# Seven biases moved off TensorE, an earlier switch of ScalarE's order, and another order for the last stores

## The chip, the cores and the metric

The kernel runs on one core of one Trainium2 chip. The metric is the device time of one execution in microseconds (us). The kernel before takes 311.48 us, the median of 3 runs (311.41 to 311.85). One execution was profiled; it took 311.45 us, and its profile spans 309.7 us from the first instruction to the last.

## The reference

There are 128 batches. Each is a matrix of 128 rows by 512 columns in 32-bit floats, and each has an integer that picks one of 10 sets of weights. The reference does this for every batch:

```python
w1 = W1[language_ids]                      # 10 x 512 x 128
w2 = W2[language_ids]                      # 10 x 128 x 512
h = einsum('bsh,bha->bsa', hidden_states, w1) + b1[language_ids][:, None, :]
h = relu(h)
adapted = einsum('bsa,bah->bsh', h, w2) + b2[language_ids][:, None, :]
x = hidden_states + adapted
normed = (x - mean(x)) * rsqrt(var(x) + 1e-05)      # over the 512 columns
return normed * gamma[language_ids][:, None, :] + beta[language_ids][:, None, :]
# and the whole is: x_in + that
```

The kernel has to form, per batch, a down-projection to 128 columns, a ReLU, an up-projection back to 512 columns, the residual sum with the bias b2, a layer norm with gamma and beta, and a second residual sum.

## The kernel before

**One batch at a time, five engines in a pipeline.** A batch fills one tile of 128 partitions by 512 columns. All weights stay in SBUF; biases, gamma and beta are spread over the 128 partitions once at the start (`spread`, L201). The main loop turns i from 3 to 129, and each turn handles several batches at different stages. With b = i - 3, a turn issues in this order:

- TensorE (PE) transposes batch i in four pieces (`transpose_x`, L234, tile pxT), multiplies batch i - 1 down (`down`, L257, tile ph) and multiplies batch i - 2 up (`up`, L274, tile py).
- GpSimd (POOL) forms r = x + b2 for batch b + 2 (`add_b2`, L244) and writes x + beta for batch b into the output tile o (`add_beta`, L251). Tile r has a ring of four buffers, o a ring of five buffers of two batches each.
- ScalarE (ACT) copies the transposed batch i out of PSUM (`copy_xT`, L238), applies the ReLU to batch i - 1 (`relu`, L265), copies the weights of batch i + 1 into place (`stage_w1`, L225), and squares batch b with a row sum (`square`, L310). After every second square it takes a reciprocal root for the pair of batches (`root`, L320).
- VectorE (DVE) adds r (or x) to py with a row sum (`residual`, L291), applies mean and gamma to an earlier batch (`scale`, L353), finishes a still earlier batch into o (`finish`, L362), and runs short steps on single columns in between (L298, L324, L326, L329).
- SyncE (SP) issues the loads of x (L71) and the stores of finished pairs (`store`, L366).

**Three ways to add b2.** In most batches GpSimd adds b2 to x ahead of time (`add_b2`) and VectorE's residual reads r. In the batches named by `b2_by_matmul` TensorE adds it, with one short matmul ahead of the up-projection into the same PSUM tile (L273), and residual reads x. In those named by `b2_by_vector` VectorE adds it to py with an instruction of its own (`vector_b2`, L284), and residual reads x.

Here B is 128 and E is B - 5 = 123. By these rules 15 batches go by matmul before (0, 1, 2, 3, 5, 9, 17, 30, 46, 62, 78, 94, 110, 121, 123), 20 by VectorE and 93 by GpSimd.

**What sets the order.** `keep` pins each engine's instructions to the order in which the program issues them; each engine works through its own list, and waits in front of an instruction whose inputs or buffers aren't ready. `stage_w1` has two places in the loop: ahead of the square from LATE on, and behind the square and the root for the batches from FIRST (8) to LATE - 1:

```python
if i + 1 >= LATE and on(i + 1):
    stage_w1(i + 1)
...
if FIRST <= i + 1 < LATE:
    stage_w1(i + 1)
```

**The tail.** From batch 124 on `tail` (L421) takes the place of the paired steps. Batches 124 to 127 get a root of their own, and each is stored on its own (`store_last`, L415). For batches 123 and 124, `by_pool` gives ScalarE the normalization (L408) and GpSimd the product with gamma (L410) and the sum with o (L412). Batch 125 is split: VectorE finishes the right 256 columns (`finish_cols`, L419), ScalarE and GpSimd the left 256 (L408, L412). Batches 126 and 127 are finished by VectorE (L419).

Of the kernel before, what the change touches and what calls it, by code (L numbers as in the profile page):

```python
# [18 lines left out]
EPS = 1e-5  # L19
FIRST = 8  # L20
EARLY = 24
LATE = 20
U = 2


# [1 line left out]
def cond_resid_kernel(ctx: ExitStack, tc: tile.TileContext, x, itok, W1, b1, W2, b2, gamma, beta, out):  # L27
# [8 lines left out]
    nc = tc.nc  # L36
    B, S, H = x.shape
# [8 lines left out]
    def keep(ins):  # L46

        engine = ins.ins.engine
        if engine in last:
            tc.add_manual_dep(ins.ins, last[engine], behind, reason="kept order")  # L50
        last[engine] = ins.ins.name
        return ins
# [14 lines left out]
    E = B - 5  # L67
# [65 lines left out]
    def lid(b, engine):  # L133
        g = b // G
        if (g, engine) not in lids:
            loads, vals = nc.values_load_multi_w_load_instructions(
                lang[0:1, g * G : (g + 1) * G],
                engines=[engine],
                min_val=0,
                max_val=L - 1,  # L140
                skip_runtime_bounds_check_because="clamped on the chip to 0..L-1 above",
            )
            for ins in loads:
                keep(ins)
            lids[g, engine] = vals
        return lids[g, engine][b % G]
# [65 lines left out]
    xT, hT, rs, os, ys, ssqs, nmeans, rstds = {}, {}, {}, {}, {}, {}, {}, {}  # L212
# [1 line left out]


    def b2_by_matmul(b):
        return b in (0, 1, 2, 3, 5, E - 2, E) or (b % 8 == 1 if b < 24 else b % 16 == 14 and b < E)

    def b2_by_vector(b):
        return 8 <= b < B - 8 and (b % 8 == 5 if b < 24 else b % 16 in (1, 6, 11))  # L220

    def stage_w1(b):
        w1s[b] = wp.tile([P, KC, A], FP, tag="w1s", name=f"w1s_{b}")
        src = (w1e if b < EARLY else w1).rearrange("p l k a -> p (l k a)")[:, bass.ds(lid(b, ET.Activation) * (KC * A), KC * A)]
        keep(nc.scalar.copy(w1s[b].rearrange("p k a -> p (k a)"), src))  # L225
# [37 lines left out]
    def relu(b):  # L263
        hT[b] = tp.tile([P, P], FP, tag="hT", name=f"hT_{b}", bufs=6)
        keep(nc.scalar.activation(hT[b], phs.pop(b), AF.Relu, bias=b1T[:, bass.ds(lid(b, ET.Activation), 1)]))  # L265
# [11 lines left out]
    def col(tiles, b):  # L277

        return tiles[b // 2][:, b % 2 : b % 2 + 1]
# [6 lines left out]
    def residual(b):  # L286
        r = rs.pop(b) if b in rs else xb(b)
        if b % 2 == 0:
            sums[b // 2] = st.tile([P, 2], FP, tag="sum", name=f"sum_{b // 2}")
        keep(  # L290
            nc.vector.scalar_tensor_tensor(ys[b], ys[b], 1.0, r, ALU.mult, ALU.add, accum_out=col(sums, b))  # L291
        )

    def negative_means(g):

        nmeans[g] = st.tile([P, 2], FP, tag="nmean", name=f"nmean_{g}")
        keep(
            nc.vector.scalar_tensor_tensor(  # L298
                nmeans[g], sums[g], -1.0 / H, ys[2 * g + 1][:, 0:2], ALU.mult, ALU.bypass
            )  # L300
        )
# [20 lines left out]
    def newton(n, ssq, t, u):  # L322
        if n == 1:
            keep(nc.vector.scalar_tensor_tensor(u, ssq, EPS * H3, t, ALU.add, ALU.mult))  # L324
        else:
            keep(nc.vector.scalar_tensor_tensor(u, u, 1.0 / H3, t, ALU.mult, ALU.mult))  # L326

    def newton_3(rstd, t, u):
        keep(nc.vector.scalar_tensor_tensor(rstd, u, -3.0, t, ALU.add, ALU.mult))  # L329
# [8 lines left out]
    def deviation(g):  # L338
        root(ssqs[g], of_pair(g)[0])

    def rstd(g, n):
        t, u = of_pair(g)
        if n < 3:
            newton(n, ssqs[g], t, u)
        else:
            rstds[g] = st.tile([P, 2], FP, tag="rstd", name=f"rstd_{g}")
            newton_3(rstds[g], t, u)
            del ssqs[g], parts_of[g]

    def scale(b):  # L350
        v = lid(b, ET.DVE)
        keep(
            nc.vector.scalar_tensor_tensor(  # L353
                ys[b], ys[b], col(nmeans, b), gamma_b[:, bass.ds(v * H, H)], ALU.add, ALU.mult
            )
        )

    def finish(b):
        g, j = divmod(b, 2)
        o = os[g][:, j, :]  # L360
        keep(
            nc.vector.scalar_tensor_tensor(o, ys.pop(b), rstds[g][:, j : j + 1], o, ALU.mult, ALU.add)  # L362
        )

    def store(g):
        keep(nc.sync.dma_start(out=out[2 * g : 2 * g + 2].rearrange("b s h -> s b h"), in_=os.pop(g)))  # L366
        del rstds[g]

    def on(b):
        return 0 <= b < B  # L370
# [5 lines left out]
    def of_one(b):  # L376
        if -b not in parts_of:
            pool, tag = {E + 3: (p_h, "h"), E + 4: (p_x, "xT")}.get(b, (p_s, "s"))
            parts_of[-b] = pool.tile([P, 1], FP, tag=tag, name=f"root_of_{b}"), st.tile([P, 1], FP, tag="part", name=f"part_of_{b}")
        return parts_of[-b]  # L380

    def rstd_of(b, n):

        t, u = of_one(b)
        if n < 3:
            newton(n, ssqs[b], t, u)
        else:
            rstds[b] = st.tile([P, 1], FP, tag="rstd", name=f"rstd_{b}")
            newton_3(rstds[b], t, u)

    def deviation_of(b):
        ssqs[b] = st.tile([P, 1], FP, tag="ssq", name=f"ssq_{b}")
        sq = tp.tile([P, H], FP, tag="sq", name=f"sq_{b}")
        keep(nc.scalar.activation(sq, ys[b], AF.Square, bias=col(sums, b), scale=-float(H), accum_out=ssqs[b]))
        root(ssqs[b], of_one(b)[0])
# [4 lines left out]
    def shift(b):  # L400
        shifts[b] = st.tile([P, 1], FP, tag="shift", name=f"shift_{b}")
        keep(nc.vector.tensor_scalar(shifts[b], col(nmeans, b), rstd_col(b), None, ALU.mult))

    def by_pool(b, scaled, cols=slice(0, H)):

        n = rp.tile([P, H], FP, tag="r", name=f"n_{b}")[:, cols]
        bias = 0.0 if scaled else shifts[b]
        keep(nc.scalar.activation(n, ys[b][:, cols], AF.Identity, bias=bias, scale=rstd_col(b)))  # L408
        if not scaled:
            keep(nc.gpsimd.tensor_tensor(n, n, gamma_b[:, bass.ds(lid(b, ET.Pool) * H, H)], ALU.mult))  # L410
        o = os[b // 2][:, b % 2, cols]
        keep(nc.gpsimd.tensor_tensor(o, n, o, ALU.add))  # L412

    def store_last(b):
        nc.sync.dma_start(out=out[b], in_=os[b // 2][:, b % 2, :])  # L415

    def finish_cols(b, cols=slice(0, H)):
        o = os[b // 2][:, b % 2, cols]
        keep(nc.vector.scalar_tensor_tensor(o, ys[b][:, cols], rstd_col(b), o, ALU.mult, ALU.add))  # L419

    def tail(b):  # L421
        p = E // 2
        residual(b)
        if b == E + 1:
            rstd(p, 1)
            scale(E - 1)
            rstd(p, 2)
            finish(E - 2)
            store(p - 1)
            rstd(p, 3)  # L430
            deviation_of(b)
            shift(E)
            by_pool(E, False)
        elif b == E + 2:
            rstd_of(b - 1, 1)
            negative_means(b // 2)
            rstd_of(b - 1, 2)
            finish_cols(E - 1)
            store_last(E - 1)
            rstd_of(b - 1, 3)  # L440
            store_last(E)
            deviation_of(b)
        elif b == E + 3:
            left, right = slice(0, H // 2), slice(H // 2, H)
            shift(b - 2)
            by_pool(b - 2, False)
            residual(b + 1)
            store_last(b - 2)
            rstd_of(b - 1, 1)
            scale(b - 1)  # L450
            rstd_of(b - 1, 2)
            negative_means(b // 2)
            deviation_of(b)
            scale(b)
            rstd_of(b - 1, 3)
            rstd_of(b, 1)
            deviation_of(b + 1)
            rstd_of(b, 2)
            scale(b + 1)
            rstd_of(b, 3)  # L460
            rstd_of(b + 1, 1)
            finish_cols(b - 1, right)
            by_pool(b - 1, True, left)
            store_last(b - 1)
            rstd_of(b + 1, 2)
            finish_cols(b)
            store_last(b)
            rstd_of(b + 1, 3)
            finish_cols(b + 1)
            store_last(b + 1)  # L470
# [46 lines left out]
    for i in range(3, B + U):  # L517
        b = i - U - 1
# [19 lines left out]
        if i > 4 and on(i - 1):  # L538
            relu(i - 1)
        if i + 1 >= LATE and on(i + 1):  # L540
            stage_w1(i + 1)
# [39 lines left out]
        if 0 <= b <= E:  # L581
            square(b)
            if half == 1:
                deviation(g)
        if FIRST <= i + 1 < LATE:
            stage_w1(i + 1)
# [41 lines left out]
```

## Time and profile before

| what | value |
|---|---|
| median of 3 runs | 311.48 us (311.41 to 311.85) |
| the profiled execution | 311.45 us, span 309.7 us |
| busy: PE | 297.2 us (96%) |
| busy: DVE | 294.7 us (95%) |
| busy: ACT | 280.5 us (91%) |
| busy: POOL | 279.6 us (90%) |
| granted TensorE clock, mean | 0.987 |
| moved by DMA | 77.59 MB, mean 251 GB/s |

The page's busy time is the union of the instructions' spans, and an instruction's span on VectorE and ScalarE laps over the start of the next one by some 0.07 to 0.1 us. So the cost of one more instruction on a full engine is the distance from its start to the start of the next one, which is a little less than the mean duration that the groups list. Four engines are above 90%, and the mean over the span doesn't tell which of them holds up the others; that has to be read from the waits and from the gaps in each engine's own timeline.

### The profile page before, as it was taken

To read this page: it belongs to the slowest core of one execution; us is meant where nothing else is said; L and a number is where in the kernel's file an instruction comes from. 1 tells how busy PE (TensorE), PEld (TensorE's weight loads), DVE (VectorE), ACT (ScalarE), POOL (GpSimd) and SP (SyncE) were. 2 spreads that over 40 slices of the span, in tenths; PEclk is the share of its full clock that TensorE was granted. 3 is DMA by queue.
4 is the path that set the end of the run, shared out by engine and by line. 5 is a ranking of instruction groups with operands and counts; after the bars stand their busy time and mean duration, and the time that the engine had idled before them with its cause. 6 is when DMAs were issued, how large, how long until landed. Compare 5 with 4: busy or idle time off the path is not lost.

```text
span 309.7 us, 6996 instructions
## 1 busy us (share of the span) xinstructions
PE 297.2 (96%) x1849; PEld 221.7 (72%) x1849; DVE 294.7 (95%) x823; ACT 280.5 (91%) x716; POOL 279.6 (90%) x234
## 2 busy tenths in 40 slices
PE   7999999999999999999999999999999999999960
PEld 3758777777777777777777777777777777777730
DVE  6787999999999999999999999999999999999994
ACT  3857999999999999999999999999999999999981
POOL 1349999988999999999999999999999999989962
PEclk9999999999999999999999999999999999999995
DMA  6999979976678666766777656667867666783334
GB/s 236 390 388 387 370 231 363 375 265 227 247 272 265 224 210 220 251 234 232 272 270 237 217 203 238 258 211 275 264 225 247 206 224 238 237 267 137 131 121 158
DMA packets 43482, 77.59 MB, mean 251 GB/s; under 512 B 1930, under 2 KB 7061, under 8 KB 43443
## 3 DMA queue, kind: packets, MB, share of 16 engines
q1 hardware_dynamic: 43382, 77.10, 71.2%
q8 instruction: 15, 0.25, 0.3%
q14 instruction: 25, 0.20, 0.2%
q10 hardware_dynamic: 60, 0.05, 0.1%
HBM read 43.58 MB, written 33.55 MB: 249 GB/s over the span
## 4 chain that ended last, share of the span: by engine, by line
PE 92%; DVE 4%; issue 1%; ACT 1%; DMA 1%; ACTq 0%; DVEq 0%
PE ph L257 36%; PE py L274 35%; PE pxT L234 18%; PE row L205 2%; PE py L273 1%; DVE py L353 1%; DVE py L291 1%; DVE o L419 1%; DMA rows<-in_L_cond_b_dram 1%; DVE b_b L210 0%; DVE left L186 0%; DVE left L184 0%; ACT sq L310 0%; DVE o L362 0%; ACT w1s L225 0%
## 5 line engine op out<-in xcount | busy, mean ns | idle before, releaser
L251 POOL TENSOR_TENSOR o<-x,beta_b 128x512 f32<-128x512 f32 x128 | 161.9, 1277 | 9.5 <-DVE beta_b L210 9.4
L257 PE MATMUL ph<-xT,w1s 128*128 128x128 f32 x1024 | 135.4, 275 | 0.0
L274 PE MATMUL py<-w,hT 128*128 x256 | 131.3, 594 | 0.2 <-ACT hT L265 0.2
L244 POOL TENSOR_TENSOR r<-x,b_b 128x512 f32<-128x512 f32 x93 | 118.7, 1276 | 11.8 <-DVE b_b L210 6.2
L257 PEld LDWEIGHTS ph<-xT,w1s 128*128 128x128 f32 x1024 | 124.9, 192 | 1.0 <-ACT hT L265 0.5
L234 PEld LDWEIGHTS pxT<-ident,x 128*128 128x128 f32 x512 | 66.3, 152 | 65.8 <-issue 35.7
L353 DVE SCALAR_TENSOR_TENSOR py<-py,nmean,gamma_b 128x512 f32<-128x512 f32 x126 | 94.9, 753 | 0.1
L310 ACT ACTIVATE sq<-py,sum 128x512 f32<-128x512 f32 x124 | 86.0, 693 | 5.4 <-DVE nmean L298 2.9
L362 DVE SCALAR_TENSOR_TENSOR o<-py,rstd,o 128x512 f32<-128x512 f32 x122 | 90.8, 744 | 0.0
L234 PE MATMUL pxT<-ident,x 128*128 128x128 f32 x512 | 78.1, 275 | 0.1
L238 ACT COPY xT<-pxT 128x512 f32<-128x512 f32 x128 | 74.7, 584 | 1.2 <-PE pxT L234 1.2
L291 DVE SCALAR_TENSOR_TENSOR py<-py,r 128x512 f32<-128x512 f32 x93 | 64.3, 692 | 2.7 <-PE py L274 1.2
L225 ACT COPY w1s<-w 128x512 f32 x104 | 64.0, 615 | 0.0
L265 ACT ACTIVATE hT<-ph,b1T 128x128 f32<-128x128 f32 x128 | 47.2, 369 | 6.6 <-PE ph L257 3.8
L274 PEld LDWEIGHTS py<-w,hT 128*128 128x128 f32 x256 | 39.9, 192 | 2.5 <-ACT hT L265 1.1
L291 DVE SCALAR_TENSOR_TENSOR py<-py,x 128x512 f32<-128x512 f32 x35 | 24.4, 697 | 2.0 <-PE py L274 0.9
L310 ACT ACTIVATION_READ_ACCUMULATOR sq<-py,sum 128x1 f32 x124 | 25.3, 204 | 0.0
L320 ACT ACTIVATE root<-ssq,eps 128x2 f32<-128x2 f32 x62 | 16.5, 266 | 2.1
L284 DVE TENSOR_TENSOR py<-py,b_b 128x512 f32<-128x512 f32 x20 | 13.8, 692 | 0.2
L291 DVE DVE_READ_ACCUMULATOR py<-py,r 128x1 f32 x93 | 13.1, 141 | 0.0
L225 ACT COPY w1s<-w1e 128x512 f32 x16 | 9.8, 611 | 1.1 <-DMA w1e<-in_L_cond_W_dram 1.1
L324 DVE SCALAR_TENSOR_TENSOR part<-ssq,root 128x2 f32<-128x2 f32 x62 | 9.3, 150 | 1.0 <-ACT root L320 1.0
(54 smaller groups left out, 99.5 us busy)
## 6 DMA issues: line engine op xcount, KB each, us to landing
out_dram<-o SPq DMA_DIRECT2D x61, 512.0 KB, 3.4
x<-in_x_dram SPq DMA_DIRECT2D x29, 1024.0 KB, 6.2
x<-in_x_dram SPq DMA_DIRECT2D x6, 512.0 KB, 8.9
w1e<-in_L_cond_W_dram SPq DMA_DIRECT2D x2, 1280.0 KB, 11.6
w<-in_L_cond_W_dram SPq DMA_DIRECT2D x4, 640.0 KB, 7.8
w1s<-in_L_cond_W_dram SPq DMA_DIRECT2D x8, 256.0 KB, 8.3
w<-in_L_cond_W_dram SPq DMA_DIRECT2D x1, 1792.0 KB, 10.1
out_dram<-o SPq DMA_DIRECT2D x6, 256.0 KB, 2.0
```

The costliest lines, as they stand in the source:

```text
L225: keep(nc.scalar.copy(w1s[b].rearrange("p k a -> p (k a)"), src))
L234: keep(nc.tensor.transpose(pxs[b][:, k, :], cols, ident))
L238: keep(nc.scalar.copy(xT[b], pxs.pop(b)))
L244: keep(nc.gpsimd.tensor_tensor(rs[b], xb(b), b2_b[:, bass.ds(v * H, H)], ALU.add))
L251: keep(nc.gpsimd.tensor_tensor(os[g][:, j, :], xb(b), beta_b[:, bass.ds(v * H, H)], ALU.add))
L257: nc.tensor.matmul(phs[b], lhsT=w1s[b][:, k, :], rhs=xT[b][:, k, :], start=(k == 0), stop=(k == KC - 1))
L265: keep(nc.scalar.activation(hT[b], phs.pop(b), AF.Relu, bias=b1T[:, bass.ds(lid(b, ET.Activation), 1)]))
L274: keep(nc.tensor.matmul(ys[b], lhsT=hT[b], rhs=w2[:, bass.ds(v * H, H)], start=not m, stop=True))
L291: nc.vector.scalar_tensor_tensor(ys[b], ys[b], 1.0, r, ALU.mult, ALU.add, accum_out=col(sums, b))
L310: nc.scalar.activation(sq, ys[b], AF.Square, bias=col(sums, b), scale=-float(H), accum_out=col(ssqs, b))
L353: nc.vector.scalar_tensor_tensor(ys[b], ys[b], col(nmeans, b), gamma_b[:, bass.ds(v * H, H)], ALU.add, ALU.mult)
L362: nc.vector.scalar_tensor_tensor(o, ys.pop(b), rstds[g][:, j : j + 1], o, ALU.mult, ALU.add)
```

## The change

Three things change.

`b2_by_matmul` keeps 0, 1, 2, 3, 5, 30, 62 and 94. The other seven leave TensorE: batches 9 and 17 go to `b2_by_vector` (13 and 21 were there already), and 46, 78, 110, 121 and 123 go to GpSimd's `add_b2`.

`LATE` falls from 20 to 12: for batches 12 to 19 the copy of the weights now comes ahead of the square instead of behind it, so ScalarE's square (and root) is the last thing of its turn.

In `tail`, in the turn of batch 126, the finish of 125's right half and GpSimd's work on its left half are issued earlier, ahead of `rstd_of(126, 3)`, `scale(127)` and `rstd_of(127, 1)`; and the store of 126 is issued ahead of that of 125. `store_last` is pinned into SyncE's order with `keep`; the other stores keep their order in the built program.

```diff
-LATE = 20
+LATE = 12
...
     def b2_by_matmul(b):
-        return b in (0, 1, 2, 3, 5, E - 2, E) or (b % 8 == 1 if b < 24 else b % 16 == 14 and b < E)
+        return b in (0, 1, 2, 3, 5) or (b % 32 == 30 and b < E)
 
     def b2_by_vector(b):
-        return 8 <= b < B - 8 and (b % 8 == 5 if b < 24 else b % 16 in (1, 6, 11))
+        return 8 <= b < B - 8 and (b % 4 == 1 if b < 24 else b % 16 in (1, 6, 11))
...
     def store_last(b):
-        nc.sync.dma_start(out=out[b], in_=os[b // 2][:, b % 2, :])
+        keep(nc.sync.dma_start(out=out[b], in_=os[b // 2][:, b % 2, :]))
...
             rstd_of(b, 2)
-            scale(b + 1)
-            rstd_of(b, 3)
-            rstd_of(b + 1, 1)
             finish_cols(b - 1, right)
             by_pool(b - 1, True, left)
-            store_last(b - 1)
-            rstd_of(b + 1, 2)
+            rstd_of(b, 3)
+            scale(b + 1)
+            rstd_of(b + 1, 1)
             finish_cols(b)
             store_last(b)
+            rstd_of(b + 1, 2)
+            store_last(b - 1)
             rstd_of(b + 1, 3)
             finish_cols(b + 1)
             store_last(b + 1)
```

## The prediction

> **What bounds the kernel now.** I read the page first: busy shares and the chain that ended last.
>
> ```profile
> PE 297.2 (96%) x1849; PEld 221.7 (72%) x1849; DVE 294.7 (95%) x823; ACT 280.5 (91%) x716; POOL 279.6 (90%) x234
> ...
> PE 92%; DVE 4%; issue 1%; ACT 1%; DMA 1%; ACTq 0%; DVEq 0%
> ```
>
> Both name TensorE, but VectorE is one point behind. So next the groups by line, for what the moved work costs on each engine, and TensorE's timeline around batch 46, which still carries its b2 matmul.
>
> ```profile
> L273 PE MATMUL py<-parts,pick 96*128 96x512 bf16 x15 | 5.7, 381 | 0.5 <-DVE b_b L210 0.5
> ...
> L284 DVE TENSOR_TENSOR py<-py,b_b 128x512 f32<-128x512 f32 x20 | 13.8, 692 | 0.2
> ...
> L244 POOL TENSOR_TENSOR r<-x,b_b 128x512 f32<-128x512 f32 x93 | 118.7, 1276 | 11.8 <-DVE b_b L210 6.2
> ```
>
> ```profile
> 119.38 0.60 PE L234 MATMUL pxT<-ident,x 128*128 128x128 f32 x4
> ...
> 120.71 0.38 PE L273 MATMUL py<-parts,pick 96*128 96x512 bf16 x1
> 120.93 1.02 PE L274 MATMUL py<-w,hT 128*128 x2
> 121.79 0.60 PE L234 MATMUL pxT<-ident,x 128*128 128x128 f32 x4
> ```
>
> From transpose to transpose this batch takes 121.79 - 119.38 = 2.41 us; one without L273 takes 2.19 (0.44 transposes, 0.89 down, 0.86 up). L273 is worth 0.22 us, start to start. Then VectorE's timeline three batches on:
>
> ```profile
> 125.78 0.74 DVE L362 SCALAR_TENSOR_TENSOR o<-py,rstd,o 128x512 f32<-128x512 f32 x1
> 126.44 0.70 DVE L291 SCALAR_TENSOR_TENSOR py<-py,r 128x512 f32<-128x512 f32 x1
> ...
> 127.78 0.74 DVE L362 SCALAR_TENSOR_TENSOR o<-py,rstd,o 128x512 f32<-128x512 f32 x1
> 128.56 0.70 DVE L284 TENSOR_TENSOR py<-py,b_b 128x512 f32<-128x512 f32 x1
> 129.17 0.15 DVE L326 SCALAR_TENSOR_TENSOR part<-part,root 128x2 f32<-128x2 f32 x1
> ```
>
> Start to start, L362 takes 0.66; only ahead of batch 49 is it 0.78, so VectorE waited 0.12 for TensorE there. A pair of batches costs VectorE 0.61 + 0.67 + 0.06 + 0.66 (even) and 0.07 + 0.62 + 0.06 + 0.67 + 0.07 + 0.66 (odd) = 4.15 us; a batch with L284 adds 0.67 (0.61 for itself and 0.06 for what follows). Sixteen batches: 8 x 4.15 + 3 x 0.67 = 35.2 on VectorE, 8 x 4.38 + 0.22 = 35.26 on TensorE. **They are balanced**: VectorE's residual starts between 0.04 and 1.0 us behind its up-projection, falls back by 0.6 at each L284 and catches up by 0.12 in each other batch. Last, GpSimd:
>
> ```profile
> POOL r L244 <- DVE py L291: 4.8, 5, 1.9
> POOL n L410 <- ACT n L408: 2.4, 1, 2.4
> ```
>
> Its idle time is a ring wait at 70.6 us (1.94), four more (0.66, 0.67, 0.69, 0.80, at 167, 203, 238 and 274 us) with one of 0.10 at 214, and 2.44 in the tail.
>
> **The change, part by part.**
>
> *TensorE.* Seven L273 go: 7 x 0.22 = 1.54 us. The Trainium skill ("Perfetto Trace Analysis", Identifying the Most-Contended Engine) says to take the engine with the highest occupancy as the bottleneck; that would make all 1.54 show and the time 309.9. The timeline decides otherwise: from 66 us on VectorE has next to no idle time, so TensorE's gain reaches the end only as far as VectorE waited for it.
>
> *VectorE up to batch 21.* Its waits for TensorE between 39 and 63 us are 0.30, 0.21, 0.15, 0.14, 0.15, 0.08, 0.30, 0.21 and 0.16: 1.70. Batches 9 and 17 add 2 x 0.67 = 1.34. They start 0.22 and 0.74 earlier than before: two L273 less, and the gaps of 0.18 and 0.12 between transposes 17 to 19 (2.40 and 2.34 for 2.22) go with `LATE`, since those copies of xT stood behind a copy of weights that stood behind a late square. Stepping the residuals forward, batch 9's ends its lag within four batches (0.57, 0.42, 0.28, 0.06), batch 17 likewise, and batch 21 comes 0.40 earlier. A further 0.47 ahead of batch 20's residual (64.97) is not TensorE's: its py was ready. Unknown; between 0 and 0.47 may vanish; I keep it.
>
> *`LATE`, its price.* The square moves behind one L225 (0.51 start to start) in eight turns. Behind it wait root and L324; from batch 20 on this order runs with one wait of L324 of 0.2 us, in the tail. Cover: VectorE's residual and scale of the next batch, 1.28 us. Cost nothing; without the cover 0.5 for each of four pairs.
>
> *VectorE from 66 us on.* Waits for TensorE of 0.12, 0.12, 0.12, 0.08 (batches 49, 65, 81, 97) and 0.11, 0.18 (123, 124) vanish: 0.73. So does most of the 0.34 ahead of L324 at 295.3, where root came late behind TensorE: 0.3. VectorE's end: 0.40 + 0.73 + 0.3 = 1.4 us earlier; L329 now directly ahead of the last L419 gives 0.07 back. Last finish from 305.33 to 304.0. TensorE, too early now, will wait for ScalarE's copies behind late squares; that starves nobody while VectorE is behind.
>
> *GpSimd.* Between 70.6 and 295.78 us it runs 180 instructions in 222.25 us busy, 1.235 each. Five more: 6.17. The idle of 2.92 (five waits after batch 46's place) is used up first; the ring wait at 70.6 hangs on VectorE's batch 22 and comes 0.40 earlier. Net: -0.40 + 6.17 - 2.92 = **+2.85 us**. Residuals 121 and 123 now wait for r, with L329 and scale queued behind; r stands 5 us or more ahead, so nothing. The skill's "GPSIMD Engine Reference", section Engine selection, speaks against this: elementwise work belongs on VectorE, GpSimd being about twice as slow. The rows have 1276 ns against 692. But by the rule five adds would cost a full VectorE 5 x 0.67 = 3.4 us (314 or so), by the rows they cost an engine that had 2.92 + 2.44 us idle. They overdraw this by a little, and it shows here:
>
> ```profile
> 292.03 3.75 POOL L251 TENSOR_TENSOR o<-x,beta_b 128x512 f32<-128x512 f32 x3
> 298.21 1.27 POOL L410 TENSOR_TENSOR n<-n,gamma_b 128x512 f32<-128x512 f32 x1 [2.44 <-ACT n L408]
> ...
> 302.13 1.26 POOL L412 TENSOR_TENSOR o<-n,o 128x512 f32<-128x512 f32 x1
> 304.33 0.72 POOL L412 TENSOR_TENSOR o<-n,o 128x256 f32<-128x256 f32 x1 [0.93 <-ACT n L408]
> ```
>
> L251 would be followed at 295.74 + 2.85 = 298.59 instead of 298.21, no longer behind ScalarE (ready by 296.8). The four steps run on: batch 124's sum ends at 303.77 (303.39), the half of 125, ready since about 302, at 304.5 (305.05).
>
> *Stores.* SyncE issued the last three like this (three lines of its timeline, and one of its waits: the kernel's end waits for three landings, 0.7 us each):
>
> ```profile
> 305.07 0.33 SPq L415 DMA_DIRECT2D out_dram<-o  x1
> 305.50 0.39 SPq L415 DMA_DIRECT2D out_dram<-o  x1
> 305.98 0.41 SPq L415 DMA_DIRECT2D out_dram<-o  x1
> SPq L623 <- DMA out_dram<-o: 2.0, 3, 0.7
> ```
>
> They land 2.0 us after the first issue, then 0.7 apart, the last at 308.5; 127's waited 0.6 behind the other two in the queue. After: 124 at 303.80, then 126, 125 and 127, which are all ready or nearly so, 0.43 to 0.47 apart; 127 at 305.1. With four in a row at 0.7 the last lands at 303.80 + 2.0 + 3 x 0.7 = 307.9. The unseen part is the fourth in a row: at issue pace (0.45) 307.2, at 0.72 308.0. I take 0.7, its own form's figure. The store order itself is worth nothing here, since the DMA engines are full from 124 on; with GpSimd early it would be worth 0.5.
>
> **Sum.** 307.9 for 308.5: -0.6 against the profiled execution's 311.45 (span 309.7, 1.75 around it), which is the median to 0.03. **310.9 us.** Its own range is 310.4 to 311.4 (start of the GpSimd run -0.9 to 0 instead of -0.4, landing pace).
>
> **Rivals.**
> 1. *The gain comes through.* Occupancy says 1.54; likewise, if GpSimd catches up, VectorE's 1.4 with the 0.5 of the store queue gives 309.5. Middle 309.8. For it: TensorE's 92% of the chain. Against: GpSimd must save 1.3 us that no row shows.
> 2. *Slower: the ring of r.* With 46, 78 and 110 in the ring, the fourth r back of 48, 80 and 112 is four batches back, not six: r can then lead its residual by at most 4 x 2.19 - 0.75 - 1.27 = 6.7 us. It led by 7.7, 8.5 and 8.7. The added instruction takes the lead to some 6.1, 6.5 and 6.7 first, so I expect no wait, but barely. If the waits return, GpSimd keeps its 2.92 of idle time: 310.9 + 2.9 = 313.8. It decides from 1.2 us of waits.
> 3. *No change.* VectorE's early waits aren't filled (batch 22 no earlier): GpSimd starts 0.4 later, 311.3; the tail hides the rest.
>
> **How the numbers follow.** 0.2% (0.62 us) is about what can be told from no change. Main case 0.51, rival 1 0.22, rival 2 0.12, rival 3 0.15. The main case straddles the bound: half faster (0.25), half same (0.26). Faster 0.25 + 0.22 = 0.47; same 0.26 + 0.15 = 0.41; slower 0.12. The range 309.7 to 311.7 leaves out rival 2 and the far end of rival 1.
>
> **What would show it.** Right: GpSimd without ring waits after 112 us, L251 running straight into L410 near 298.6, 0.93 gone ahead of the last L412, VectorE's last L419 ending near 304.0, four stores landing 0.7 apart. TensorE shows waits of its transposes for L238. Wrong: L244 waiting for L291 late; L419 ending after GpSimd; L324 waiting for L320 around 50 us; VectorE waiting for TensorE after 66 us.

## The result, and the profile after

The changed kernel takes **310.83 us** (median of 11 runs, 310.51 to 311.35) beside 311.56 us for the kernel before on the same chip (11 runs, 311.34 to 311.88). The ratio is **0.9977**, interval [0.9968, 0.9987]: faster by 0.7 us, or 0.23%, just over what can be told from no change. The profiled execution took 310.83 us, its span is 309.1 us, its granted clock 0.987 as before.

The page of the kernel after, its busy times and the chain that ended last, by engine:

```profile
PE 295.1 (95%) x1842; PEld 220.2 (71%) x1842; DVE 294.8 (95%) x825; ACT 280.4 (91%) x716; POOL 285.5 (92%) x239
...
PE 56%; POOL 28%; issue 10%; POOLq 2%; DVE 1%; DMA 1%; ACTq 0%; DVEq 0%
```

TensorE lost 2.1 us of busy time, GpSimd gained 5.9, VectorE stands. In the chain GpSimd, which had no share worth a listing before, now holds 28%. Followed back from the last instruction, the chain stays on GpSimd, with the issue times between its instructions, as far as 181 us, and only the part before that runs on TensorE; and yet TensorE and VectorE are still the two busiest engines.

The groups of the kernel after that carry b2, of GpSimd, VectorE and TensorE (operation, shapes, count; then busy us and mean ns of one; then idle time just before them):

```profile
L244 POOL TENSOR_TENSOR r<-x,b_b 128x512 f32<-128x512 f32 x98 | 126.3, 1288 | 8.8 <-DVE b_b L210 6.2 <-DVE py L291 1.7 <-DMA x<-in_x_dram 0.6
...
L284 DVE TENSOR_TENSOR py<-py,b_b 128x512 f32<-128x512 f32 x22 | 15.3, 695 | 0.1
...
L273 PE MATMUL py<-parts,pick 96*128 96x512 bf16 x8 | 3.0, 380 | 0.5 <-DVE b_b L210 0.5
```

L244 went from 93 to 98 instructions, L284 from 20 to 22, L273 from 15 to 8. Of the 11.8 us that GpSimd had stood idle ahead of L244, 8.8 are left, and of these only 1.7 are waits for VectorE's residual (L291), which frees the buffers of r.

TensorE's timeline of the kernel after at batch 46 (start, duration, both in us), and then VectorE's ahead of batch 49, the two places that the prediction had read in the kernel before:

```profile
118.78 0.60 PE L234 MATMUL pxT<-ident,x 128*128 128x128 f32 x4
119.22 1.06 PE L257 MATMUL ph<-xT,w1s 128*128 128x128 f32 x8
120.11 1.02 PE L274 MATMUL py<-w,hT 128*128 x2
120.98 0.60 PE L234 MATMUL pxT<-ident,x 128*128 128x128 f32 x4
```

```profile
127.18 0.75 DVE L362 SCALAR_TENSOR_TENSOR o<-py,rstd,o 128x512 f32<-128x512 f32 x1
127.84 0.70 DVE L284 TENSOR_TENSOR py<-py,b_b 128x512 f32<-128x512 f32 x1
128.44 0.16 DVE L326 SCALAR_TENSOR_TENSOR part<-part,root 128x2 f32<-128x2 f32 x1
```

L273 is gone and the batch takes 120.98 - 118.78 = 2.20 us (2.41 before). VectorE goes from L362 to L284 in 0.66 us (0.78 before): the wait of 0.12 is gone.

GpSimd after 66 us: its waits of the kernel after (engine, instruction, what it waited for: us in total, times, the longest), all that are listed; and its timeline, at the longer of the two waits and then in the tail, where a bracket would show idle time ahead of an instruction.

```profile
POOL r L244 <- DVE py L291: 1.7, 2, 1.5
```

```profile
70.04 1.28 POOL L244 TENSOR_TENSOR r<-x,b_b 128x512 f32<-128x512 f32 x1 [1.47 <-DVE py L291]
...
294.88 3.72 POOL L251 TENSOR_TENSOR o<-x,beta_b 128x512 f32<-128x512 f32 x3
298.57 1.26 POOL L410 TENSOR_TENSOR n<-n,gamma_b 128x512 f32<-128x512 f32 x1
299.91 1.26 POOL L412 TENSOR_TENSOR o<-n,o 128x512 f32<-128x512 f32 x1
301.13 1.27 POOL L410 TENSOR_TENSOR n<-n,gamma_b 128x512 f32<-128x512 f32 x1
302.48 1.95 POOL L412 TENSOR_TENSOR o<-n,o 128x512 f32<-128x512 f32 x2
```

From 70.04 us on GpSimd is idle for 0.37 us in all before the tail. The first L410 follows the last L251 with no wait; before, it stood 2.44 us waiting for ScalarE and started at 298.21. The half of batch 125 follows batch 124's sum at once (the last row holds both); its wait of 0.93 is gone. GpSimd ends at 302.48 + 1.95 = 304.43. VectorE, whose timeline ends with this line, is through 0.74 us earlier, at 303.69 (before: 305.33, after GpSimd):

```profile
302.94 0.75 DVE L419 SCALAR_TENSOR_TENSOR o<-py,rstd,o 128x512 f32<-128x512 f32 x1
```

SyncE's part of the timeline has the first of the last four stores (batch 124) and the last (batch 127); the waits of SyncE's queue show the landings that the end waits for:

```profile
303.77 0.33 SPq L415 DMA_DIRECT2D out_dram<-o  x1
...
305.17 0.40 SPq L415 DMA_DIRECT2D out_dram<-o  x1
```

```profile
SPq L415 <- POOL o L412: 5.8, 2, 3.6
SPq L623 <- DMA out_dram<-o: 2.2, 3, 0.9
```

Store 124 waits for GpSimd's sum (L412), and the other three follow at issue pace, at 304.19, 304.67 and 305.17. They land at 305.78, 306.50, 307.18 and 307.90; before, the last landed at 308.5.

### The profile page after: what moved, and what is told of

Same layout as the page of the kernel before. It is cut to its first block, busy times and chain, and to the rows that moved or that the text cites. A ratio compares the mean times of both kernels' runs of the same rounds, so it can differ in the third digit from the quotient of the medians.

```text
span 309.1 us, 6983 instructions
## 1 busy us (share of the span) xinstructions
PE 295.1 (95%) x1842; PEld 220.2 (71%) x1842; DVE 294.8 (95%) x825; ACT 280.4 (91%) x716; POOL 285.5 (92%) x239
## 4 chain that ended last, share of the span: by engine, by line
PE 56%; POOL 28%; issue 10%; POOLq 2%; DVE 1%; DMA 1%; ACTq 0%; DVEq 0%
PE ph L257 22%; PE py L274 21%; POOL o L251 17%; PE pxT L234 11%; POOL r L244 9%; PE row L205 2%; POOLq L136 1%; POOL n L410 1%; POOL o L412 1%; POOLq L244 1%; PE py L273 1%; DMA rows<-in_L_cond_b_dram 1%; DVE b_b L210 0%; POOLq L623 0%; DVE left L186 0%
## 5 line engine op out<-in xcount | busy, mean ns | idle before, releaser
L251 POOL TENSOR_TENSOR o<-x,beta_b 128x512 f32<-128x512 f32 x128 | 163.3, 1288 | 9.4 <-DVE beta_b L210 9.4
L244 POOL TENSOR_TENSOR r<-x,b_b 128x512 f32<-128x512 f32 x98 | 126.3, 1288 | 8.8 <-DVE b_b L210 6.2
L362 DVE SCALAR_TENSOR_TENSOR o<-py,rstd,o 128x512 f32<-128x512 f32 x122 | 91.1, 747 | 0.0
L238 ACT COPY xT<-pxT 128x512 f32<-128x512 f32 x128 | 74.7, 584 | 1.2 <-PE pxT L234 1.2
L291 DVE SCALAR_TENSOR_TENSOR py<-py,r 128x512 f32<-128x512 f32 x98 | 68.0, 694 | 1.5 <-PE py L274 1.1
L291 DVE SCALAR_TENSOR_TENSOR py<-py,x 128x512 f32<-128x512 f32 x30 | 21.0, 698 | 1.6 <-issue 0.9
L284 DVE TENSOR_TENSOR py<-py,b_b 128x512 f32<-128x512 f32 x22 | 15.3, 695 | 0.1
L291 DVE DVE_READ_ACCUMULATOR py<-py,r 128x1 f32 x98 | 14.1, 144 | 0.0
L324 DVE SCALAR_TENSOR_TENSOR part<-ssq,root 128x2 f32<-128x2 f32 x62 | 9.5, 153 | 0.9 <-ACT root L320 0.8
```

Of the source, the lines that this page charges most:

```text
L238: keep(nc.scalar.copy(xT[b], pxs.pop(b)))
L244: keep(nc.gpsimd.tensor_tensor(rs[b], xb(b), b2_b[:, bass.ds(v * H, H)], ALU.add))
L251: keep(nc.gpsimd.tensor_tensor(os[g][:, j, :], xb(b), beta_b[:, bass.ds(v * H, H)], ALU.add))
```

## The experiments

Two theories were tested. **A**, the prediction's: in the changed kernel GpSimd's list, which runs almost without idle time from about 70 us to its end, sets the end of the kernel; each addition on it costs some 1.2 us, and the 1.6 to 1.7 us that TensorE and VectorE are earlier lie hidden behind it. **B**: TensorE (or VectorE, which it feeds) still sets the end; GpSimd's list has room. Every ratio below is to the kernel before on the same chip. "Batch 127's residual" stands for VectorE's progress.

### One or two additions back on TensorE

From the changed kernel, 123 alone, or 121 and 123, return to the matmul (E is 123).

```diff
 def b2_by_matmul(b):
-    return b in (0, 1, 2, 3, 5) or (b % 32 == 30 and b < E)
+    return b in (0, 1, 2, 3, 5, E) or (b % 32 == 30 and b < E)
```

> The changed kernel, with batch 123 alone back on TensorE. Theory: GpSimd is shorter by one addition, 1.235 us, and still the last; its product for batch 123 starts near 297.3, the store of batch 124 goes out near 302.5, four stores land 0.7 us apart, the last near 306.7: 1.2 us below the changed kernel, 309.6. Rival (TensorE): 0.22 above, 311.05. Rival (tail order): 310.8.

```diff
-    return b in (0, 1, 2, 3, 5) or (b % 32 == 30 and b < E)
+    return b in (0, 1, 2, 3, 5, E - 2, E) or (b % 32 == 30 and b < E)
```

> The changed kernel, with batches 121 and 123 back on TensorE's short matmul. Theory (GpSimd's list sets the end): GpSimd has two additions fewer, 2.47 us, and is ready for batch 123's product before ScalarE is; the product starts near 296.6 us instead of 298.57, batch 124's store is issued near 301.8, VectorE's last finish (303.7) now sets the end, and the last store lands near 306.0 instead of 307.9. About 1.8 us below the changed kernel: 309.0 us. Rival (TensorE sets the end, by its 95% busy): two short matmuls more, 0.44 us above the changed kernel: 311.3. Rival (the gain was the tail's order alone): unchanged, 310.8.

Measured: with 123 back 309.81 us (309.13 to 310.03), ratio **0.9929** [0.9915, 0.9944]; with both 309.40 us (309.21 to 310.25), ratio **0.9926** [0.9912, 0.9939]. Giving work back to the busiest engine makes the kernel faster by another 0.5%, which is A; under B it would have been slower. The changed kernel's ratio is 0.9977. GpSimd in the tail, with 123 back, and with both back:

```profile
297.69 1.32 POOL L410 TENSOR_TENSOR n<-n,gamma_b 128x512 f32<-128x512 f32 x1
```

```profile
297.16 1.27 POOL L410 TENSOR_TENSOR n<-n,gamma_b 128x512 f32<-128x512 f32 x1 [0.74 <-ACT n L408]
```

With one back, L410 still runs straight on. Its unbroken run began 0.39 us later in that execution than in the changed kernel's (70.43 for 70.04) and lasted 227.26 us for 228.53: one addition less, 1.27 us less. With two back GpSimd waits 0.74 us for ScalarE again: it no longer sets the end, and the second addition brings next to nothing. What sets it then is VectorE, in the last line of its timeline:

```profile
303.61 0.75 DVE L419 SCALAR_TENSOR_TENSOR o<-py,rstd,o 128x512 f32<-128x512 f32 x1
```

It ends at 304.36, where I had taken it to stay near 303.7. The two matmuls' 0.44 us is back on TensorE, and in its wake the waits of 0.11 and 0.18 at 123 and 124 and one of 0.20 of L324 for root; counted from batch 8's residual, batch 127's is 1.17 us earlier than before instead of 1.72. So the last landing came at 306.71 and not at 306.0, and the time was 0.4 over the expected one.

### One more addition on GpSimd

```diff
-    return b in (0, 1, 2, 3, 5) or (b % 32 == 30 and b < E)
+    return b in (0, 1, 2, 3, 5) or b in (30, 62)
```

> The changed kernel, with batch 94 moved from TensorE to GpSimd as well. Theory: GpSimd is longer by one addition, 1.235 us, less 0.06 us of a wait near 259 us that it eats: the product of batch 123 starts near 299.7 and the end is 1.2 us above the changed kernel, 312.0. Rival (TensorE): 0.22 us below it, 310.6.

Measured 312.21 us (311.78 to 312.70), ratio **1.0012** [1.0003, 1.0021]. TensorE has 0.22 us less to do and the kernel is slower than the changed one, and slower than before. The tail of GpSimd and the end of VectorE in this run:

```profile
296.49 3.77 POOL L251 TENSOR_TENSOR o<-x,beta_b 128x512 f32<-128x512 f32 x3
300.16 1.32 POOL L410 TENSOR_TENSOR n<-n,gamma_b 128x512 f32<-128x512 f32 x1
```

```profile
303.29 0.75 DVE L419 SCALAR_TENSOR_TENSOR o<-py,rstd,o 128x512 f32<-128x512 f32 x1
```

GpSimd runs straight through and reaches L410 at 300.16 (its run is 1.07 us longer than the changed kernel's), while VectorE is through at 304.04, 2.0 us ahead of GpSimd's end (304.13 + 1.94 = 306.07). From two additions fewer to one more, the end follows GpSimd's count, not TensorE's or VectorE's.

### The five additions on VectorE instead

From the changed kernel, 46, 78, 110, 121 and 123 go to VectorE.

```diff
 def b2_by_vector(b):
-    return 8 <= b < B - 8 and (b % 4 == 1 if b < 24 else b % 16 in (1, 6, 11))
+    return b in (46, 78, 110, E - 2, E) or (8 <= b < B - 8 and (b % 4 == 1 if b < 24 else b % 16 in (1, 6, 11)))
```

> The changed kernel with batches 46, 78, 110, 121 and 123 on VectorE instead of GpSimd. Theory: VectorE has no idle time there, so its last finish moves from 303.7 us by five times 0.67, some 3.3 us, to 307.0, the last store lands near 309.1 instead of 307.9: 1.2 us above the changed kernel, a ratio of 1.002 to the kernel before. GpSimd is then far ahead and waits for its ring. Rival (the addition takes half as long on VectorE, so it belongs there): below the changed kernel, a ratio under 0.9977.

Measured 312.51 us (ten of 12 runs 311.84 to 313.16, two of 316.3), ratio 1.0023 [0.9997, 1.0049]. The profiled execution, one of the two, began 3.88 us late, already there at batch 8's residual, so only differences within it are read: VectorE arrives at batch 127 3.47 us later than in the changed kernel (expected 3.3, five additions of 0.67), and the last landing is 1.6 us later. GpSimd waits for VectorE and ScalarE again:

```profile
POOL r L244 <- DVE py L291: 5.9, 8, 1.5
POOL n L410 <- ACT n L408: 2.4, 1, 2.4
POOL r L244 <- DVE rstd L329: 1.2, 2, 0.6
```

By mean duration an addition costs 695 ns on VectorE and 1288 ns on GpSimd, and yet five of them are about 1.5 us dearer on VectorE (1.0023 for 0.9977), since VectorE had no idle time and GpSimd had 5.

### The tail's order, taken out and put in alone

First the changed kernel with the old order of the tail (the `keep` of `store_last` stays):

```diff
             rstd_of(b, 2)
-            finish_cols(b - 1, right)
-            by_pool(b - 1, True, left)
-            rstd_of(b, 3)
             scale(b + 1)
+            rstd_of(b, 3)
             rstd_of(b + 1, 1)
+            finish_cols(b - 1, right)
+            by_pool(b - 1, True, left)
+            store_last(b - 1)
+            rstd_of(b + 1, 2)
             finish_cols(b)
             store_last(b)
-            rstd_of(b + 1, 2)
-            store_last(b - 1)
```

> The changed kernel with the tail's order of the kernel before (scale of 127 ahead of the right half of 125, GpSimd's half of 125 after it, stores 125, 126, 127). Theory: nothing changes, 310.8, since from batch 124's store on the stores only follow one another, whichever comes first, and GpSimd is the last in either order. Rival (the order is what gained): back to the kernel before, 311.5.

Measured 311.06 us (ten of 11 runs 310.80 to 311.51, one of 314.8, which draws the ratio up), ratio 0.9986 [0.9964, 1.0009]: no difference from the changed kernel's 0.9977 that can be told. In the traces (one execution each), GpSimd's unbroken run began 0.375 us later here (70.42 for 70.04); with that taken off, the last landing is 307.93, and 307.90 in the changed kernel. Nothing, as expected, but not because all the stores behind 124's are ready, as had been supposed. In the old order 125's store waits for GpSimd's half of 125; GpSimd's last line and this store:

```profile
302.87 1.95 POOL L412 TENSOR_TENSOR o<-n,o 128x512 f32<-128x512 f32 x2
```

```profile
304.84 0.33 SPq L415 DMA_DIRECT2D out_dram<-o  x1
```

GpSimd ends at 302.87 + 1.95 = 304.82, and the store goes out 0.68 us behind 124's (304.16) instead of 0.42. The stores land some 0.7 us apart in either order (here at 306.19, 306.89, 307.58 and 308.30), so a store issued 0.26 us later lands no later.

Then the kernel before with only the new tail:

```diff
-        nc.sync.dma_start(out=out[b], in_=os[b // 2][:, b % 2, :])
+        keep(nc.sync.dma_start(out=out[b], in_=os[b // 2][:, b % 2, :]))
...
-            scale(b + 1)
-            rstd_of(b, 3)
-            rstd_of(b + 1, 1)
             finish_cols(b - 1, right)
             by_pool(b - 1, True, left)
-            store_last(b - 1)
-            rstd_of(b + 1, 2)
+            rstd_of(b, 3)
+            scale(b + 1)
+            rstd_of(b + 1, 1)
             finish_cols(b)
             store_last(b)
+            rstd_of(b + 1, 2)
+            store_last(b - 1)
```

> The kernel before with the new order of the tail and nothing else. Theory (the order is worth something only while GpSimd is early): GpSimd's half of batch 125 starts straight behind batch 124's sum, near 303.4 us instead of 304.33; stores go out as 126 near 304.3, 125 near 304.8, 127 near 305.45 instead of 305.98, and the last lands near 307.75 instead of 308.5: 0.75 us faster than before, a ratio of 0.9976. So the tail alone would give as much as the whole change, and the parts don't add up. Rival (the tail's order is worth nothing, as it is in the changed kernel): a ratio of 1.000.

Measured 311.08 us (310.66 to 311.65), ratio **0.9972** [0.9955, 0.9990]. GpSimd's last line, and SyncE's store of batch 127:

```profile
302.97 2.09 POOL L412 TENSOR_TENSOR o<-n,o 128x512 f32<-128x512 f32 x2
```

```profile
306.28 0.33 SPq L415 DMA_DIRECT2D out_dram<-o  x1
```

The half of 125 now runs straight behind 124's sum; the stores go out at 304.26, 305.16 (126), 305.59 (125) and 306.28 (127), so 127 is issued as soon as VectorE is done with it (305.50 + 0.75 = 306.25) and waits behind nothing. Batch 127's residual came 0.83 us later in this execution than in the profile of before, but the last landing only 0.08 later: the new tail saves 0.75 us. **On its own, the tail's order is worth as much as the whole change, and inside the change nothing that these runs can tell.**

### LATE alone, and batches 9 and 17 alone

Both from the kernel before.

```diff
-LATE = 20
+LATE = 12
```

> The kernel before with the weights' copy ahead of the square from batch 12 on, and nothing else. Theory: the gaps of 0.18 and 0.12 us between the transposes of batches 17 to 19 go, and with them 0.3 us of VectorE's waits; TensorE and VectorE stay balanced behind it, so the end comes 0.3 us earlier, a ratio of 0.999. Rival (the square's delay holds up the roots and so VectorE): 0.5 us per pair in four pairs, up to 2 us slower, a ratio up to 1.006.

```diff
-    return b in (0, 1, 2, 3, 5, E - 2, E) or (b % 8 == 1 if b < 24 else b % 16 == 14 and b < E)
+    return b in (0, 1, 2, 3, 5, E - 2, E) or (b == 1 if b < 24 else b % 16 == 14 and b < E)
...
-    return 8 <= b < B - 8 and (b % 8 == 5 if b < 24 else b % 16 in (1, 6, 11))
+    return 8 <= b < B - 8 and (b % 4 == 1 if b < 24 else b % 16 in (1, 6, 11))
```

> The kernel before with batches 9 and 17 on VectorE instead of TensorE, and nothing else. Theory: VectorE has 1.34 us more, filled into 1.7 us of waits for TensorE, which itself is 0.44 us early but then waits longer for ScalarE's copies behind later squares, since those still come ahead of the weights' copy: VectorE ends 0.1 us earlier, between 0.3 earlier and 0.3 later: a ratio of 1.000. Rival (TensorE sets the time): 0.44 us faster, 0.9986.

LATE alone: 311.53 us (310.96 to 311.97), ratio 0.9981 [0.9964, 0.9997]. The transposes of batches 18 and 19 in this run's TensorE timeline, and then in that of the kernel before:

```profile
53.19 0.63 PE L234 MATMUL pxT<-ident,x 128*128 128x128 f32 x4
...
55.41 0.63 PE L234 MATMUL pxT<-ident,x 128*128 128x128 f32 x4
```

```profile
52.92 0.74 PE L234 MATMUL pxT<-ident,x 128*128 128x128 f32 x4
...
55.26 0.63 PE L234 MATMUL pxT<-ident,x 128*128 128x128 f32 x4
```

2.22 us for 2.34: the gaps ahead of the transposes are gone, here and at 17. Counted from batch 8's residual, TensorE is 0.31 us earlier from batch 20 to batch 127, and VectorE, 0.49 earlier at batch 24, is 0.31 earlier from batch 40 on.

9 and 17 alone: 311.33 us (311.05 to 311.95), ratio 0.9973 [0.9949, 0.9998]. I had expected no change, give or take 0.3. Counted from batch 8's residual, both engines are 0.13 us earlier from batch 40 to batch 82 and 0.28 at batch 127, the early end of that. The two intervals reach close to 1 and both stand on a change of 0.3 us in the trace.

Alone, tail, LATE and these two batches give 0.75 + 0.31 + 0.28 = 1.34 us by the traces; with the five batches on GpSimd added, 0.6 is left. The parts don't add up, since three of them speed VectorE and its stores, and the fourth makes GpSimd later than VectorE.

### LATE = 9 on the faster versions

Gaps between the transposes of batches 9 to 11 and 22 to 27 were still to be seen, so LATE was lowered once more, on the version with 123 back and on that with both back.

> The changed kernel with batch 123 back on TensorE and the weights' copy ahead of the square from batch 9 on, not 12. Theory: the gaps between the transposes of batches 9 to 11 (2.33, 2.34 and 2.26 for 2.22, 0.2 us together) shrink, TensorE, VectorE and the start of GpSimd's unbroken run at 70 us all come up to 0.2 us earlier, and so does the end: 0.2 us below the run with batch 123 back alone, a ratio to the kernel before of 0.9923. Rival (early gaps are hidden behind GpSimd's ring): no change, 0.9929.

> The changed kernel with batches 121 and 123 back on TensorE and the weights' copy ahead of the square from batch 9 on. Theory: up to 0.2 us below the run with 121 and 123 back alone, where VectorE behind TensorE sets the end: a ratio to the kernel before of 0.992. Rival: no change, 0.9926.

Measured 309.56 us (309.38 to 309.68), ratio 0.9931 [0.9918, 0.9944], and 309.61 us, ratio 0.9941 [0.9920, 0.9962]: neither is better than 0.9929 and 0.9926 without it. In the first, TensorE's timeline still has the gaps from batch 8 to batch 11:

```profile
30.03 0.63 PE L234 MATMUL pxT<-ident,x 128*128 128x128 f32 x4
...
32.40 0.75 PE L234 MATMUL pxT<-ident,x 128*128 128x128 f32 x4
...
34.74 0.68 PE L234 MATMUL pxT<-ident,x 128*128 128x128 f32 x4
...
37.01 0.63 PE L234 MATMUL pxT<-ident,x 128*128 128x128 f32 x4
```

2.37, 2.34 and 2.27 us where the pace is 2.22 (those at 22 to 27 are gone): these gaps don't come from the order of square and copy, as I had thought. In the second all are 2.22 behind batch 8, but batch 8 itself started 0.8 us later. The traces name what they do come from. In the first, ScalarE's timeline has this wait:

```profile
31.25 0.62 ACT L225 COPY w1s<-w1e 128x512 f32 x1 [1.06 <-DMA w1e<-in_L_cond_W_dram]
```

ScalarE's first copy of weights, for batch 8, waits until 31.25 us for a load of the weights; its copy of batch 8's xT stands behind it, and the next transposes wait for that copy. In the second the copy of the weights starts at nearly the same time, 31.10, but TensorE and ScalarE are themselves later by then: ScalarE's wait is 0.15 and the gaps are gone. The run with `LATE` alone has the same (transposes of batch 8 at 30.76, a wait of 0.30, none of these gaps). No edit moved the load, so this is read from traces and not tested.

## Why the prediction was right, point by point

The time (310.9 predicted, 310.83 measured), its sign and its main reason hold: TensorE's gain stays hidden, and GpSimd's list sets the end. Step by step:

- **TensorE, 7 x 0.22 = 1.54: right.** Its work on batch 127 comes 1.72 us earlier than before, of the 1.54 + 0.31 (LATE's, by its run alone) that had been taken from it. Some small gaps came up in its place: 2.32 and 2.24 us ahead of the transposes of batches 23 and 27, and 2.46 us for batch 62, which keeps its matmul (2.41 before; batch 94's 2.46 is the 2.47 of before).
- **The occupancy rule** of the Trainium skill's "Perfetto Trace Analysis" (Identifying the Most-Contended Engine), as the prediction applied it, gave 309.9. The section does name the engine with the highest occupancy, but it excepts TensorE: there it asks for MFU and the busy share of the weight loads (72% here) in place of matmul busy time. So the 309.9 rests on a 96% that the section does not use for TensorE, and by the weight loads' share VectorE, at 95%, would come first. Neither of the two decided: TensorE lost its 1.54 us, VectorE ended 1.64 us earlier, and the kernel gained 0.7, since GpSimd, fourth of the four at 90% before and now at 92%, ended last.
- **VectorE's end, -1.4: mis-sized, and its sum came as near as it did partly by luck.** It ended 1.64 us earlier (303.69 for 305.33); its residual at batch 127 came 1.72 earlier, so nearly all of TensorE's 1.54 + 0.31 = 1.85 came through. At batch 24 it was 0.57 earlier, where the prediction had 0.40 from batch 21 on: by batch 19 it had gained only 0.08, and 0.48 came at batch 20, where the unexplained wait of 0.47 ("I keep it") didn't recur. From there to batch 127 it gained 1.15, for 0.73 + 0.3, by other terms than those summed. Ahead of batches 49, 81, 123 and 124 the waits went as said (0.13, 0.12, 0.11, 0.19). Ahead of 65 and 97, three batches behind 62 and 94, which keep their matmul, it gained 0.04 and nothing for 0.12 and 0.08. The wait of L324 gave 0.13 for 0.3. And two pauses that had not been counted, ahead of the residuals of batches 85 and 112, went as well (0.18 and 0.21). Like the 0.47, they stood before residuals whose py and r had been ready for 0.3 us or more; what they were stays open. From 66 us on the page of waits lists none for VectorE, as said. The error didn't reach the time, since VectorE isn't what ends last.
- **LATE at no cost: right**, and alone it is worth 0.31 us.
- **GpSimd, +2.85: right.** L410 began at 298.57 (predicted 298.59). The terms: the ring wait near 70 us ended 0.57 us earlier (0.40 predicted); from there GpSimd took 228.56 us for 185 instructions with 0.37 idle, 1.233 each (1.235 before). So 0.57 earlier, 3.39 longer, together +2.82 for L251's end. That this comes within 0.03 us of the +2.85 is luck: the start came 0.17 earlier than predicted, 0.37 of the idle time stayed that was to be used up, and the slightly quicker pace took off some 0.23. 124's store left at 303.77 (303.80), the half of 125 ended at 304.43 (304.5).
- **No ring waits: nearly.** Three came, at 118.4, 188.8 and 259.2 us, of 0.23, 0.09 and 0.06: rival 2's mechanism at its three places, in a small form: r leads its residual by 6.16 us there, where the prediction had put the ceiling at 6.7. Their 0.37 us are far from the 1.2 from which it would have decided.
- **Stores, last landing at 307.9: right** (307.90). The unseen fourth store in a row landed 0.72 us behind the third, like the others. That the order of 125 and 126 is worth nothing that can be told inside this change is shown by its undoing; that it would be worth 0.5 with an early GpSimd was low, as the tail's order alone gave 0.75, of which the store of 127 is a part.
- **The GpSimd rule** of the Trainium skill's "GPSIMD Engine Reference" (Engine selection) would have the five additions on VectorE, which came out some 1.5 us slower than on GpSimd, although the rows agree with the page's factor of about two for one addition (1288 for 695 ns). The prediction costed them at 3.4 us on VectorE, 314 us or so; they measured 312.51. VectorE was 3.47 later than in the changed kernel, so the price per addition was right; but of this 1.72 had been gained by the rest of the change, and only about 1.75 over the kernel before was left.
- **Rival 1 fell**: GpSimd saved nothing beyond its waits. With one or two additions fewer the gain does come through (309.8 and 309.4 for rival 1's 309.8), which is the same mechanism seen from the other side: the change overdraws GpSimd's idle time by about one addition (with 123 alone back, VectorE's last finish ends at 304.26 us and its store goes out at 304.34, so the two engines are about level).

I said TensorE would now wait for ScalarE's copies of xT. Its weight loads' waits for L238 rose from 22.7 to 26.2 us in all, after 66 us; the batch at 118.78 above shows none of it in its 2.20 us.

The best version is the changed kernel with 123, or 121 and 123, left on TensorE: 0.9929 and 0.9926, faster than both kernels, and not to be told from each other.

## What to carry to other kernels

When several engines are over 90% busy, an engine's idle time is a budget: add up its waits (here 2.9 us in the ring and 2.4 in the tail), subtract what a move adds (five additions, 6.2 us), and stop moving before it is overdrawn; the engine with the lowest occupancy becomes the last one sooner than its share suggests. Price a moved instruction by start-to-start distance on the engine that receives it, and against that engine's own waits, not by which engine runs it faster. Test the parts of a change alone: a part that is worth the whole gain by itself (the tail's order) may be worth nothing beside a part that moves the end elsewhere.

## What the runs showed of the hardware

- The start of a program is not the same in each execution. Batch 8's residual began between 37.24 and 37.73 us in eleven of these twelve profiles, and at 41.13 in one; all that follows is shifted by it. In eight of them it began 6.02 to 6.04 us behind ScalarE's first copy of weights, which waits for a load by DMA until 31.22 to 31.47 us. A few tenths of a microsecond between two executions' spans are thus no finding, and traces that differ by so little are compared from a common early point.
- GpSimd's 512-column additions kept the same pace, 1.233 us each, through 185 in a row with 0.37 us of pauses; its mean duration rose from 1276 to 1288 ns with fewer pauses between them, while the distance from start to start did not rise.
- Four stores of 256 KB, issued 0.42 to 0.50 us apart, landed 0.68 to 0.72 us apart, the first 2.0 us after its issue. Meanwhile (305.4 to 307.0 us) the 16 DMA engines were busy 98% of the time or more and moved 375 to 386 GB/s, which is 256 KB in 0.7 us. Issuing faster than that brought nothing, and only the moment of the first of an unbroken row counted.
